# Top-k attentions: a chunk's negated maxima transposed and added one chunk's step sooner than its weights

## The chip, the cores and the metric

The kernel runs on one core of a Trainium2 chip. Times are device microseconds of one execution. The kernel before was run three times: 2546.03 us is the median, 2543.44 and 2556.37 us are the ends. One execution was profiled, and it has a time of its own.

## What is computed

Eight sequences of 256 tokens with 128 features go through four layers. Each layer adds a gated cross-attention and a gated feed-forward part to `x`:

```python
x = x + tanh(g_xattn[n]) * xattn_n(layernorm(x), ctx)
x = x + tanh(g_ffn[n])   * ffn_n(layernorm(x))
```

The cross-attentions are, in order: a causal linear attention with random features (block 0), an attention with 8 heads of 64 that keeps the 64 largest of 256 scores of a query (block 1), a full attention with 16 heads of 8 (block 2), and an attention with 16 heads of 8 that keeps the 32 largest of 256 scores (block 3). The feed-forward parts are a full attention beside eight linear experts (block 0), gated experts (block 1), eight experts with GELU and a shared one (block 2), and an attention whose projections are mixtures of 16 experts (block 3). The change touches the two attentions that keep the largest scores:

```python
sim = q @ k.T * scale                       # per head: 256 queries x 256 keys
keep = the k largest of each query          # k = 64 (block 1), 32 (block 3)
attn = softmax(where(keep, sim, -inf))
out = attn @ v
```

## The kernel before

The 2048 tokens are worked on in four groups of 512 (two sequences each). The program is emitted by two Python generators side by side. `largest_scores` emits block 1's cross-attention and then block 3's, for all four groups. `others` emits all the other blocks in the list that `stages` gives. A group's part of block 3's attention may start only when `block2_ffn` has finished that group (`middle`), and block 1's only when `block0_ffn` has (`started`). The last feed-forward blocks (`block3_ffn`) follow block 3's attention.

Both attentions are emitted by `attention_largest`. It works in chunks: a sequence's heads are split in four, so there are 32 chunks for each of the two attentions. For chunk k there are these steps:

- `fetch` (L412) multiplies queries and keys on PE (L420), with queries on the partitions, and copies the scores from PSUM into SBUF on ACT (L427).
- The search finds out which scores are dropped. In block 3 (`largest`, L376) DVE takes the eight largest of a row (L385) and replaces them (L389), four times over for each of eight rows of heads and query halves, which is 32 maxima and 24 replacements in a chunk. POOL takes the first maximum with its sign changed (L387) and makes a mask of what lies below the last one (L392). In block 1 a threshold is found by counting signs on ACT (`count`, L495), and DVE picks from what lies near it (`keep_largest`, L536 to L558), one step later.
- `weigh` (L563) makes the weights with keys on the partitions. First `shifted` brings the negated maxima to where they are needed. In block 3 (L1378) two transposes on PE put them into a PSUM bank (L1382), and DVE adds them to the chunk's queries (L1383); the queries have a row for it, against which the keys hold a one. In block 1 (L1192) two products transpose them in three bf16 parts (L1198), and ACT copies them to a row in SBUF (L1204). Then PE multiplies keys and queries again (L574), adds block 1's row (L582) and subtracts the mask (L584) into the same PSUM tiles; ACT counts the mask (L592, block 3) and takes the exponential (L599); and PE multiplies with the values (L357 or L1216).

The loop at L652 emits a step k: the search of chunk k with the fetch of chunk k + 1 (`units`, L620) and, spread between its pieces, the weights of chunk k - 2, which `behind` holds. An `Ahead(steps, gen)` (L31) takes its pieces in proportion to the share of the step that is done. Before the change `weigh` yields after the shift, after the exponentials and after the products, so the shift of a chunk is emitted at the start of a step, its score products after a quarter, its output products after a half.

What is emitted is not yet the order of execution. The whole program stands in a block with `schedule_with_timeline_sim=True` (L1845): a planner with costs of its own lays out the order of each engine's instructions from the emitted order and the dependencies. Each engine then works through its own list in that order, and waits where an operand is not there.

PSUM is handed out in two kinds of tiles: four of one bank (`bank`, L110), which hold the transposed maxima among others, and two of two banks (`pair`, L113), which hold the scores of `fetch`, the weights of `weigh`, and those of blocks 0 and 2.

Other lines that the prediction names: the outputs of full attentions and of block 3's attention are divided on DVE (L347), transposed (L341 ahead of it and L324 behind it) and projected (L330); `block1_ffn` multiplies an expert's gated half (L1273) by a routing weight (L1301) on DVE and then multiplies with the second matrix on PE (L1303); the layer norm's last step is L275 on DVE and its transposes are L282; `block2_ffn` multiplies on PE at L1476 and L1445; `block3_ffn` at L1580 to L1582.

Of the kernel before, what the change touches and what calls it, by code (L numbers as in the profile page):

```python
# [30 lines left out]
class Ahead:  # L31
# [18 lines left out]
    def finish(self):  # L50
        while self.step():
            pass
        return self.value


def alongside(gen, *others):

    for f in gen:
        for o in others:
            o.up_to(f)  # L60
        yield f
    for o in others:
        o.finish()
# [27 lines left out]
def gated_blocks_kernel(ctx: ExitStack, tc: tile.TileContext, a, out):  # L91
# [9 lines left out]
    def program(exact):  # L101
# [11 lines left out]
        def pair(name="pair"):  # L113
            return psum.tile([P, 1024], F32, tag="pair", name=name, bufs=2)

        def work(name):

            return act.tile([P, 1024], F32, tag="work", name=name, bufs=4)
# [277 lines left out]
        def attention_largest(  # L396
# [9 lines left out]
            NP = R // 2  # L406
            NJ = 2 * R
            batches = [(g, bb) for g in groups for bb in range(2)]
            ready, ahead, masks, shifts, placed = {}, {}, {}, {}, {}
            n = len(batches) * 4  # L410

            def fetch(k):  # L412
# [117 lines left out]
            def keep_largest(k):  # L530
# [25 lines left out]
                for j in range(NJ):  # L556
# [3 lines left out]
                        accum_out=dropped[:, NJ * k + j : NJ * k + j + 1],  # L560
                    )

            def weigh(k):  # L563

                i, c = divmod(k, 4)
                qT, kT, va = ready[i]
                mask = masks.pop(k)
                row = shifted(shifts.pop(k), qT, c)
                yield
                sps = [pair("sw").rearrange("p (r n q) -> p r n q", r=2, n=2) for _ in range(NP)]  # L570
                for m in range(2):
                    for r in range(R):
                        rs = slice(rows * r, rows * r + rows)
                        nc.tensor.matmul(  # L574
                            sps[r // 2][:, r % 2, m, :], lhsT=kT[rs, c, m * P : (m + 1) * P], rhs=qT[rs, c, :],
                            start=(m == 0), stop=False,
                        )
                for r in range(R):
                    for m in range(2):
                        sp = sps[r // 2][:, r % 2, m, :]  # L580
                        if row is not None:
                            nc.tensor.matmul(sp, lhsT=pick[:, r : r + 1].to_broadcast([P, P]), rhs=row, start=False, stop=False)  # L582
                        for qc in range(2):
                            nc.tensor.matmul(  # L584
                                sp[:, qc * P : (qc + 1) * P], lhsT=mask[:, r, qc, m * P : (m + 1) * P], rhs=drop,
                                start=False, stop=(m == 1 and qc == 1),
                            )
                if dropped is not None and not search:

                    for h in range(NP):  # L590
                        kept = act.tile([P, NJ // NP, S], BF16, tag="s", name="kept", bufs=2)
                        nc.scalar.activation(  # L592
                            kept, mask[:, 2 * h : 2 * h + 2].rearrange("p r q k -> p (r q) k"), AF.Copy,
                            accum_out=dropped[:, NP * k + h : NP * k + h + 1],
                        )
                es = []
                for sp in sps:
                    e = work("eK").rearrange("p (r n q) -> p r n q", r=2, n=2)
                    nc.scalar.activation(e, sp, AF.Exp)  # L599
                    es.append(e)  # L600
                yield
                products(i, c, es, va)
                yield
                if c == 3:
                    yield from finish(i, *batches[i])

            behind = Ahead(0, iter(()))
# [4 lines left out]
            def look_ahead(k, share):  # L612

                i = k // 4 + 1
                if k < n and i < len(batches) and k % 4 >= first_of and i not in ready and may_start(batches[i][0]):
                    if i not in ahead:
                        ahead[i] = Ahead(9, prepare(*batches[i]))
                    ahead[i].up_to((k % 4 - first_of + share) / (last_of - first_of + 0.5))

            def units(k):  # L620
                if not search:
                    for r in range(R):
                        if k < n:
                            for u, _ in enumerate(select(k, r)):
                                yield (r + (u + 1) / (2 * rounds)) / R
                        if r == R - 2 and k + 1 < n:
                            yield from until_ready(k + 1)
                            fetch(k + 1)
                        yield (r + 1) / R
                    return  # L630
                for slot in range(4):
                    parts = []
                    if k < n:
                        if slot == 0:
                            parts.append(first(k))
                        elif slot % 2:
                            parts.append(count(k, slot // 2))
                        elif k + 1 < n:
                            yield from until_ready(k + 1)
                            fetch(k + 1)  # L640
                    if 0 < k <= n:
                        if slot % 2 == 0:
                            parts.append(count(k - 1, 2 + slot // 2))
                        elif slot == 3:
                            parts.append(keep_largest(k - 1))
                    for u in range(5):
                        for p in parts:
                            next(p, None)
                        yield (slot + (u + 1) / 5) / 4

            steps = n + 2
            for k in range(steps):  # L652
                for f in units(k):
                    if f is not None:
                        behind.up_to(f)
                        look_ahead(k, f)
                    yield None if f is None else (k + f) / steps
                behind.finish()

                done = k - 1  # L660
                if 0 <= done < n:
                    behind = Ahead(4 if done % 4 < 3 else 12, weigh(done))
            for _ in alongside((x / 12 for x in range(1, 13)), behind):
                yield 1.0

# [213 lines left out]
        for g in range(NG):  # L879
# [6 lines left out]
            for t in range(NT):  # L886
                n = g * NT + t
# [267 lines left out]
        def block1_xattn(groups, room, dropped, may_start, done):  # L1155
# [73 lines left out]
            def finish(i, g, bb):  # L1229
# [10 lines left out]
                if bb == 1:  # L1240
                    done.add(g)

            yield from attention_largest(
                groups, prepare, shift, shifted, products, finish, 64, 8, room, dropped, not exact, may_start
            )
# [122 lines left out]
        def block3_xattn(groups, weights, rounds, room, dropped, may_start, finished):  # L1368
# [25 lines left out]
            def finish(i, g, bb):  # L1394
                yield from heads_back(g, bb, oTs.pop(i), done)
                if bb == 1:
                    finished.add(g)

            yield from attention_largest(
                groups, prepare, shift, shifted, products, finish, 32, rounds, room, dropped, False, may_start  # L1400
            )
# [486 lines left out]
```

## Time and profile before

| | |
|---|---|
| median of three runs | 2546.03 us |
| profiled execution, its own time | 2546.42 us |
| its span in the profile | 2544.7 us |
| mean granted clock of TensorE | 0.862 |
| PE, matrix products busy | 2123.7 us (83%) |
| DVE busy | 1762.5 us (69%) |
| ACT busy | 1149.0 us (45%) |
| POOL busy | 879.8 us (35%) |
| block 3's maxima (L385), first and last | 1192.5 and 2347.4 us |

The span is what the profile sees; the rest of the execution's time lies around it. PE is TensorE, DVE is VectorE, ACT is ScalarE, POOL is GpSimd. In the row of slices the span is cut into 40 equal parts of 63.6 us, and a digit is the busy share of a part in tenths (9 is 90% or more). The chain is followed back from the last instruction to what released each step; a share of it tells where time was set. A line of waits has the engine and tile that waited, what it waited for, then the total in us, the times and the longest. A line of a timeline has the start, the length, the engine, line and operands, and in brackets the idle time ahead of it with what ended it. A fp32 product shows as several matrix records, so the counts of PE are higher than the counts of calls.

### The profile page before, as it was taken

What the parts mean: (1) busy time and instruction counts of PE and PEld (TensorE: products, weight loads), DVE (VectorE), ACT (ScalarE), POOL (GpSimd) and SP (SyncE); (2) the same over time, 40 slices, a digit from 0 to 9 for tenths busy, and PEclk for the clock granted to TensorE, in tenths of its full rate; (3) what the DMA queues carried; (4) which work ended last, traced back from release to release, by engine and by line L of the source; (5) the groups of instructions that cost most, each with busy time, mean ns of one, the idle gap of its engine ahead of it and who ended that gap; (6) DMA issues with size and microseconds to landing.
All of it is one profiled execution on the core that took longest, in us unless ns stands there. A gap on an engine that the chain in (4) does not pass through costs nothing.

```text
span 2544.7 us, 35734 instructions
## 1 busy us (share of the span) xinstructions
PE 2123.7 (83%) x12068; PEld 1292.4 (51%) x12094; DVE 1762.5 (69%) x5463; ACT 1149.0 (45%) x2437; POOL 879.8 (35%) x2252
## 2 busy tenths in 40 slices
PE   7998888887878778888989868899676975988898
PEld 5655455554445444445444435445343444666677
DVE  4635757756765667665899879894798869798332
ACT  2236556546554677864355433464333542322101
POOL 3104434434432464531334324341233334233000
PEclk8999889978988889998599966899775986999999
DMA  2000001000000000010001100021000110000000
GB/s 63 6 1 2 1 1 32 1 1 1 1 1 1 1 26 1 26 34 22 1 1 42 34 1 1 1 59 50 1 1 1 42 42 1 1 5 1 5 5 6
DMA packets 47896, 32.97 MB, mean 13 GB/s; under 512 B 4747, under 2 KB 42838, under 8 KB 47702
## 3 DMA queue, kind: packets, MB, share of 16 engines
q1 hardware_dynamic: 47702, 30.58, 4.2%
q8 instruction: 97, 1.59, 0.3%
q14 instruction: 97, 0.79, 0.1%
HBM read 29.53 MB, written 1.05 MB: 12 GB/s over the span
## 4 chain that ended last, share of the span: by engine, by line
DVE 39%; PE 36%; ACT 13%; POOL 8%; issue 4%; DMA 0%; DVEq 0%; SPq 0%; ACTq 0%; POOLq 0%
DVE m L385 13%; DVE wk L389 12%; ACT signs L495 4%; PE sm L687 3%; PE sw L723 3%; PE ph L1476 3%; PE pp L299 3%; PE y L1445 2%; DVE nmz L695 2%; PE po L1635 2%; ACT sign L495 2%; PE oT L357 2%; PE o L1216 2%; DVE xe L851 2%; DVE list L542 1%
## 5 line engine op out<-in xcount | busy, mean ns | idle before, releaser
L392 POOL TENSOR_SCALAR mask<-rooms,m 128x256 bf16<-128x256 f32 x192 | 223.3, 1163 | 385.5 <-DVE m L385 353.4
L385 DVE MAX8 m<-wk 128x8 f32<-128x256 f32 x768 | 326.8, 426 | 37.0 <-DVE wk L389 0.9
L723 PE MATMUL sw<-qT,kT 32*128 32x256 f32 x1024 | 172.4, 476 | 68.3 <-ACT eK L599 24.1
L695 DVE TENSOR_REDUCE nmz<-sm 128x4 f32<-128x1024 f32 x128 | 154.9, 1219 | 105.1 <-PE sm L687 96.6
L389 DVE MATCH_REPLACE8 wk<-m,wk 128x256 f32<-128x256 f32 x512 | 208.9, 408 | 0.0
L495 ACT ACTIVATE signs<-room,nt 128x256 bf16<-128x256 f32 x288 | 145.9, 507 | 128.7 <-POOL nt L527 78.5
L687 PE MATMUL sm<-kT,qT 32*128 32x256 f32 x1024 | 152.6, 440 | 40.0 <-DVE nmz L695 28.4
L592 ACT ACTIVATE kept<-mask 128x1024 bf16<-128x1024 bf16 x64 | 67.6, 1057 | 227.3 <-POOL mask L392 227.1
L1476 PE MATMUL ph<-xnT,we 128*128 128x512 f32 x288 | 156.2, 638 | 15.5 <-ACT hT L1477 7.4
L723 PEld LDWEIGHTS sw<-qT,kT 32*128 32x128 f32 x1024 | 101.0, 222 | 128.4 <-DVE nmz L695 32.3
L737 ACT ACTIVATE eT<-sw 128x1024 f32<-128x1024 f32 x128 | 129.6, 1019 | 79.9 <-PE sw L723 73.9
L574 PE MATMUL sw<-qTk,kTk 32*128 32x256 f32 (+1 forms) x768 | 120.8, 456 | 53.6 <-DVE qTk L1383 35.2
L1445 PE MATMUL y<-hT,we 128*128 128x512 f32 x288 | 146.0, 620 | 0.6 <-DVE wb_sb L1457 0.6
L687 PEld LDWEIGHTS sm<-kT,qT 32*128 32x128 f32 x1024 | 92.3, 205 | 101.0 <-DVE nmz L695 42.9
L1477 ACT ACTIVATE hT<-ph,b 128x512 f32<-128x512 f32 x144 | 98.4, 686 | 98.8 <-PE ph L1476 94.4
L599 ACT ACTIVATE eK<-sw 128x1024 f32<-128x1024 f32 x96 | 96.6, 1019 | 89.4 <-PE sw L584 88.5
L420 PE MATMUL sp<-kTk,qTk 32*128 32x256 f32 (+1 forms) x768 | 121.1, 448 | 14.8 <-ACT eT L737 6.5
L357 PE MATMUL oT<-eT,va 128*32 128x256 f32 x1024 | 120.6, 449 | 10.2 <-ACT eT L737 9.3
L392 POOL TENSOR_SCALAR mask<-room,m 128x256 bf16<-128x256 f32 x64 | 74.5, 1164 | 155.2 <-DVE m L385 152.8
L574 PEld LDWEIGHTS sw<-qTk,kTk 32*128 32x128 f32 (+1 forms) x768 | 71.5, 212 | 96.1 <-issue 42.4
L420 PEld LDWEIGHTS sp<-kTk,qTk 32*128 32x128 f32 (+1 forms) x768 | 72.5, 209 | 59.5 <-issue 17.0
L387 POOL TENSOR_SCALAR nmk<-m 128x1 f32<-128x1 f32 x256 | 59.5, 232 | 100.7 <-DVE m L385 100.6
(381 smaller groups left out, 4976.2 us busy)
## 6 DMA issues: line engine op xcount, KB each, us to landing
we<-in_L_ffn_exp_w_dram SPq DMA_DIRECT2D x64, 256.0 KB
we<-in_L_ffn_shared_w_dram SPq DMA_DIRECT2D x8, 256.0 KB
x<-in_x_dram SPq DMA_DIRECT2D x4, 256.0 KB
big_ctx<-in_ctx_dram SPq DMA_DIRECT2D x4, 256.0 KB
w1f<-in_L_ffn_fc_w_dram SPq DMA_DIRECT2D x1, 1024.0 KB
w3a<-in_L_ffn_q_proj_dram SPq DMA_DIRECT2D x4, 256.0 KB
w3a<-in_L_ffn_k_proj_dram SPq DMA_DIRECT2D x4, 256.0 KB
w3b<-in_L_ffn_v_proj_dram SPq DMA_DIRECT2D x4, 256.0 KB
```

The costliest lines, as they stand in the source:

```text
L357: nc.tensor.matmul(o[32 * r : 32 * r + 32, :], lhsT=va[:, n, 4 * c + r, :], rhs=es[r // 2][:, r % 2, n, :], start=(n == 0), stop=(n == 1),)
L385: nc.vector.max(m8, src[:, j, :])
L389: nc.vector.match_replace(wk[:, j, :], m8, src[:, j, :], LOWEST)
L392: nc.gpsimd.tensor_scalar(mask[:, j, :], s[:, j, :], m8[:, 7:8], 1.0, ALU.is_lt, ALU.mult)
L420: nc.tensor.matmul(sps[r // 2][:, r % 2, qc, :], lhsT=qT[rs, c, qc * P : (qc + 1) * P], rhs=kT[rs, c, :], start=(qc == 0), stop=(qc == 1),)
L495: nc.scalar.activation(to, s[:, j, :], AF.Sign, bias=nt[:, j : j + 1], accum_out=acc[:, j : j + 1])
L574: nc.tensor.matmul(sps[r // 2][:, r % 2, m, :], lhsT=kT[rs, c, m * P : (m + 1) * P], rhs=qT[rs, c, :], start=(m == 0), stop=False,)
L687: nc.tensor.matmul(sps[r // 2][:, r % 2, j, :], lhsT=qT[rs, 2 * cp + j, qc * P : (qc + 1) * P], rhs=kT[rs, 2 * cp + j, :], start=(j == 0), ...
L695: nc.vector.tensor_reduce(nmz[:, qc, 2 * cp : 2 * cp + 2, 2 * h : 2 * h + 2, 8].rearrange("p c r -> p r c"), sps[h], AX.X, ALU.max, negate ...
L723: nc.tensor.matmul(sps[r // 2][:, r % 2, n, :], lhsT=kT[rs, c, n * P : (n + 1) * P], rhs=qT[rs, c, :], start=(n == 0), stop=(n == 1),)
L1445: nc.tensor.matmul(y, lhsT=w2[:, c, :], rhs=hs[c // 2][:, js], start=(c == 0), stop=(c == 3))
L1476: nc.tensor.matmul(pp[:, js], lhsT=w1[:, c * P : (c + 1) * P], rhs=xnT, start=True, stop=True)
```

## The change

A new function `shift_scores` calls `shifted` for the chunk whose search has just ended, one step before its weights. The loop calls it once the share of the step is over 0.6, or at the end of the step. `weigh` no longer calls `shifted` and no longer yields behind it, so `Ahead` counts 3 pieces (11 at the end of a sequence) instead of 4 (12): the score products of the chunk come at the start of the following step, the output products after a third. The operations and their operands stay the same.

```diff
+            def shift_scores(k):
+
+                if 0 <= k < n:
+                    i, c = divmod(k, 4)
+                    rows_of[k] = shifted(shifts[k], ready[i][0], c)
+
             def weigh(k):
 
                 i, c = divmod(k, 4)
                 qT, kT, va = ready[i]
                 mask = masks.pop(k)
-                row = shifted(shifts.pop(k), qT, c)
-                yield
+                shifts.pop(k)
+                row = rows_of.pop(k)
...
             for k in range(steps):
                 for f in units(k):
                     if f is not None:
+                        if f > 0.6 and k - 1 not in rows_of:
+                            shift_scores(k - 1)
                         behind.up_to(f)
                         look_ahead(k, f)
                     yield None if f is None else (k + f) / steps
+                if k - 1 not in rows_of:
+                    shift_scores(k - 1)
                 behind.finish()
 
                 done = k - 1
                 if 0 <= done < n:
-                    behind = Ahead(4 if done % 4 < 3 else 12, weigh(done))
+                    behind = Ahead(3 if done % 4 < 3 else 11, weigh(done))
```

More of the change, by code (lines that the diff above doesn't have):

```diff
@@ L408, in attention_largest @@
             batches = [(g, bb) for g in groups for bb in range(2)]
-            ready, ahead, masks, shifts, placed = {}, {}, {}, {}, {}
+            ready, ahead, masks, shifts, placed, rows_of = {}, {}, {}, {}, {}, {}
             n = len(batches) * 4
```

## The prediction

> **What bounds the kernel now.** I read the page first (shares and slices, then the chain), then the waits of the matrix engine, then stretches of the span, then the matrix engine's timeline where it stood idle.
>
> ```profile
> span 2544.7 us, 35734 instructions
> PE 2123.7 (83%) x12068; PEld 1292.4 (51%) x12094; DVE 1762.5 (69%) x5463; ACT 1149.0 (45%) x2437; POOL 879.8 (35%) x2252
> ...
> PE   7998888887878778888989868899676975988898
> ...
> DVE  4635757756765667665899879894798869798332
> ...
> DVE m L385 13%; DVE wk L389 12%; ACT signs L495 4%; PE sm L687 3%; PE sw L723 3%; PE ph L1476 3%; PE pp L299 3%; PE y L1445 2%; DVE nmz L695 2%; PE po L1635 2%; ACT sign L495 2%; PE oT L357 2%; PE o L1216 2%; DVE xe L851 2%; DVE list L542 1%
> ```
>
> No engine is the bound throughout. Up to 1140 us (18 slices of 63.6) PE is mostly 80 to 90% busy and the chain is mixed. From 1192 us, where block 3's search starts, the chain changes hands: a group's eight chunks of maxima run at DVE's pace (slices at 8 and 9; L385 and L389 are a quarter of the whole chain), then the next group waits until block 2's experts (`block2_ffn`), on PE, have finished it. The gaps in DVE's maxima show it: 1450 to 1482, 1729 to 1797, 2039 to 2071 us, each ahead of a new group.
>
> ```profile
> PE sw L574 <- DVE qTk L1383: 35.2, 8, 10.6
> PE pt_o L324 <- DVE o_sb L347: 33.0, 13, 8.2
> ```
>
> The first line is what the change aims at: block 3's weight products waited eight times, 35.2 us in all, for the addition of the shift. PE takes its products in order, so all behind them waits as well. The largest, at 1490.8, 1806.0 and 2078.5 us, are 10.6, 9.0 and 7.4 us, the last chunks of groups 0, 1 and 2.
>
> **The change, part by part.** No operation is added or removed. 64 transposes (L1382) and 32 additions (L1383, 0.41 us) of block 3, and 64 products (L1198) and 32 copies (L1204, 0.34 us) of block 1, are emitted at 0.6 of the step before; the weights lose one of their paces, so scores, mask products and exponentials come a quarter step sooner, the outputs a sixth. No DMA moves, POOL gets nothing new. A planner then sets each engine's order, and that of the changed program can be read without running it. To price places in it I count the instructions ahead and use the trace of before: one maximum with its share of the replacement costs 0.84 us (chunk 16, 1797.5 to 1824.4 us, 26.9 us for 32).
>
> (1) *The waits aimed at.* The additions of chunks 7, 15 and 23 pass only 4, 3 and 4 maxima (278 to 274 ahead, 533 to 530, 785 to 781), while their weights on PE stay: 3.4, 2.5 and 3.4 us of 27.0, since these chunks' shift comes at 0.6 of a step whose maxima can't start sooner. The other five waits are 8.2 us together; most go. So at most some 16 of 35.2 us. And what follows takes it back:
>
> ```profile
> 1525.25 0.47 PE L324 MATMUL pt_o<-ident,o_sb 128*128 128x128 f32 x1 [8.18 <-DVE o_sb L347]
> ```
>
> 24 us after the 10.6 us wait PE waits again, for an output in DVE's queue with 307 maxima ahead of it (306 in the new order). DVE is 88% busy from 1480 to 1530 us (44.1 of 50), so a PE that comes 3.4 us sooner waits 3.4 us longer. Bounds -16 and 0; I take -2, near the lower end of the gain, because two of the three large waits lie in such stretches.
>
> (2) *A new lag in group 0.* The price of the change is in the vector queue. In the new order block 3's maxima of chunks 2 to 5 stand ahead of other work there: the last eight multiplications by routing weights (L1301) of `block1_ffn` for group 2 have 114 to 142 maxima ahead instead of 94 to 121 (17 to 24 more), the normalization (L275) of `block2_ffn` for group 1 has 161 instead of 137 to 139. At 0.84 us that is 14 to 20 us; with what else changed places, each at its own row's mean, 12 to 19; I take 15. PE's order hardly moves there (those products L1303 have -2 to +5 us more PE work ahead), and in before it arrives with nothing to spare:
>
> ```profile
> 1297.73 1.12 PE L1303 MATMUL y<-h,w1f 128*128 128x512 f32 x2 [0.22 <-DVE h L1301]
> ...
> 1323.42 1.88 PE L1303 MATMUL y<-h,w1f 128*128 128x512 f32 x2 [2.50 <-DVE h L1273]
> ```
>
> The same place shows in block 3's own weights: for chunks 2, 3 and 4 they come 4 to 16 us of PE work sooner while the additions come 2 to 5 us of DVE work later, which turns 0.2 to 2.8 us to spare into lacks of 8 to 16. These are one lag, not several: PE runs 15 us ahead of DVE there and has to give that up once. Behind it in PE's queue is `block2_ffn` of group 1, whose end opens block 3's group 1.
>
> ```profile
> 1282.00:1325.00 43.00, 38.51 (x163) 18.87 (x164) 41.25 (x152) 20.26 (x28) 14.13 (x23) 0.94 0.00 1
> 1325.00:1480.00 155.00, 142.86 (x688) 73.40 (x689) 129.30 (x389) 81.05 (x124) 56.62 (x78) 0.93 0.11 31
> 1697.00:1797.00 100.00, 94.79 (x473) 50.69 (x472) 53.56 (x121) 51.34 (x80) 20.66 (x24) 0.97 0.13 38
> 1960.00:2057.00 97.00, 91.66 (x315) 41.75 (x317) 63.51 (x215) 50.75 (x73) 34.31 (x47) 0.92 0.20 55
> ```
>
> (Stretch, length, then busy us of PE, weight loads, DVE, ACT, POOL; then the granted clock.) From 1325 to 1480 us PE is idle for 12.1 of 155 us, so it can win back little: bounds 0 (all absorbed) and +15; I take +12 at the start of group 1 (1482 us in before).
>
> [...]
>
> ```profile
> 1480.00:1490.80 10.80, 10.20 (x98) 5.59 (x90) 7.87 (x26) 4.99 (x5) 3.79 (x7) 1.00 0.01 2
> 1490.80:1501.40 10.60, 0.04 (x2) 0.03 (x1) 9.77 (x33) 3.23 (x5) 4.07 (x6) 0.67 0.00 0
> 1501.40:1512.00 10.60, 9.86 (x47) 5.84 (x47) 9.74 (x33) 2.40 (x4) 4.07 (x6) 0.50 0.00 0
> ```
>
> After 10.6 us of waiting the granted clock was 0.50 for at least the next 10.6: 9.86 us of work that takes 4.93 at full clock, 4.9 us lost. [...]
>
> (3) *A gain in group 2.* The outputs of `block2_xattn` for group 3 (L347) and the normalization of its experts (L275) pass 10 maxima: 701 to 691 ahead, 8.4 us. PE waits there for both (5.33 and 3.63 us below, 0.91 and 1.75 between them), and 94% of the stretch behind it (1960 to 2057) is PE work that opens group 3.
>
> ```profile
> 1947.95 0.47 PE L324 MATMUL pt_o<-ident,o_sb 128*128 128x128 f32 x1 [5.33 <-DVE o_sb L347]
> ...
> 1960.46 1.38 PE L282 MATMUL pt_ln<-ident,xn 128*128 128x128 f32 x4 [3.63 <-DVE xn L275]
> ```
>
> Bounds -8.4 and 0, since the outputs also need transposes (L341) that PE issues no sooner; I take -5.
>
> (4) *Block 1.* Its three waits for the row copy (4.2 us) go, covered by more work between copy and use; mask products come up to 16 us nearer to the masks (L558), which 14 of them already waited for (8.3 us). Bounds -4 and +8, taken at 0: products of scores and searches keep their places. One more activation-table load in all (1.28 us) lies on ACT, 45% busy; uncovered it would cost its length.
>
> (5) *The last group.* The fetch of chunk 26 falls behind 14 of the first 16 experts of `block3_ffn` for group 0: 42 products of about 0.43 us are 18 us of delay for that chunk. In before the next chunk has such a gap (2158.8 to 2180.7 us), and in the new order it goes, as chunk 27's fetch keeps its place. Taken at 0, bounds 0 and +18. The products after 2350 us keep their order to 4 us.
>
> Sum: -2 + 12 - 5 + 0 + 0 = +5. On the profiled execution's own 2546.42 us (span 2544.7, 1.7 around it) that is 2551.4; this execution stands 0.4 above the median of the three runs, 2546.03. I say 2551.
>
> **The rivals.** *Slower, by one mechanism:* the lag of (2) is paid whole and with the half clock. 19.9 us, nothing won back, is about 2566. For it: PE's 92% from 1325 us on. Against it: 12 us of idle there, and (3). It decides from 12.7 us on. *Faster:* PE's waits go and the next groups really open sooner: -16 from (1), -8 from (3), and only 6 of the lag remains: 2528. For it: PE is 92 to 95% busy ahead of each opening. Against it: 8.18 us at 1525. *The change does nothing,* since the three large waits stay: 2546; for it, DVE's order of maxima itself moves by 1% at most. It counts with my own case.
>
> **How the numbers follow.** 0.5%, 12.7 us, is about what a measurement of this kernel can tell from no change. My case, with the one that nothing happens: 0.38, its own range 2540 to 2558. Slower: 0.37, 2559 to 2590, with (4) and (5) at their upper ends. Faster: 0.25, 2515 to 2533. 2524 to 2580 leaves out a tenth at each end.
>
> **What would show it.** Right: waits of L574 for L1383 fall to about 20 us, with those of chunks 7, 15 and 23 still there; PE waits more for L1301 or L1273 around 1285 to 1340 us; group 1's first maximum some 10 us later than 1482, group 3's within 6 us of 2071. Wrong: group 1 starts at or before 1482, or the time from 2071 to the end (473 us) moves by more than 8 us.

## The result and the profile after

| | before | after |
|---|---|---|
| median | 2548.71 us (7 runs) | 2562.33 us (7 runs, 2555.25 to 2570.18) |
| ratio, 95% interval | | 1.0051 (1.0033 to 1.0068) |
| span of the profiled execution | 2544.7 us | 2560.6 us |
| its mean granted clock | 0.862 | 0.861 |

The changed kernel is slower by 0.5%, 13.6 us between the medians; the prediction said 5 us. Its range (2524 to 2580) holds the time, but the range is wide: 2562.33 us lies outside that of the prediction's own case (2540 to 2558) and in that of its slower rival (2559 to 2590). In the changed kernel the lines of `weigh` are six further down (L574 is L580) and those behind the loop ten (L1383 is L1393); in the variants with a condition it is thirteen and seventeen. The page of the changed kernel answers to the one of before:

```profile
span 2560.6 us, 35742 instructions
PE 2111.6 (82%) x12067; PEld 1290.8 (50%) x12094; DVE 1760.7 (69%) x5463; ACT 1150.9 (45%) x2438; POOL 878.7 (34%) x2252
...
PE   7999789788878778888689968899776966778898
...
DVE  4535767856754767655999679894789766997332
...
DVE m L385 12%; DVE wk L389 11%; ACT signs L495 6%; PE y L1455 3%; PE sm L697 3%; PE ph L1486 3%; PE pp L299 3%; PE sw L733 3%; ACT sign L495 2%; PE o L1226 2%; PE po L1645 2%; DVE nmz L705 2%; PE pqk L1590 2%; PE pqk L1591 2%; PE pv L1592 2%
```

The work is the same, DVE's maxima still lead the chain, and `block3_ffn`'s products (L1590 to L1592) have come into its list: this fits time that has gone to the last group. The waits of PE in the changed kernel (total, times, longest):

```profile
PE o L1226 <- ACT eK L605: 38.5, 17, 4.2
PE pt_o L324 <- DVE o_sb L347: 29.4, 13, 7.7
...
PE sw L580 <- ACT rooms L427: 19.6, 4, 8.3
...
PE sw L580 <- DVE qTk L1393: 5.4, 3, 3.5
```

The wait that the change aims at fell from 35.2 to 5.4 us by its name. It did not go, though: 19.6 us now stand under the copy of fetched scores (L427), which was not among the weights' costly waits before. All waits of L574 (L580 after), whatever for, went from 53.5 to 47.7 us. And in block 1 the output products wait 38.5 us for the exponentials (L1216: 14.6 before).

The first maximum of a chunk marks the stages (us from the start of the span, one execution each):

| first maximum of | before | after | difference |
|---|---|---|---|
| chunk 0 (end of block 1's search) | 1192.5 | 1196.8 | +4.3 |
| chunk 8 (group 1) | 1482.3 | 1489.9 | +7.6 |
| chunk 16 (group 2) | 1797.5 | 1807.6 | +10.1 |
| chunk 24 (group 3) | 2071.1 | 2075.6 | +4.5 |
| chunk 26 | 2127.9 | 2154.8 | +26.9 |
| chunk 27 | 2180.7 | 2187.7 | +7.0 |
| last maximum ends | 2347.4 | 2357.5 | +10.1 |
| span | 2544.7 | 2560.6 | +15.9 |

Group 2 gives 5.6 us back; from group 3's first maximum to the end 473.6 us have become 485.0, and PE's busy time there is about the same, so it is idle for 98.0 us instead of 85.0 (before's line first):

```profile
2071.10:2544.70 473.60, 388.59 (x2206) 305.59 (x2206) 302.31 (x903) 97.06 (x194) 97.91 (x160) 0.89 0.01 3
```

```profile
2075.60:2560.60 485.00, 387.04 (x2206) 304.50 (x2206) 302.74 (x903) 97.07 (x193) 98.15 (x160) 0.88 0.01 3
```

That is the place that the prediction took at nothing. Its waits of PE (from 2181 us in before, 2188 us in the changed kernel, to the last maximum) show new names. The changed kernel:

```profile
PE pt_e L1620 <- ACT e L1616: 9.0, 2, 8.1
...
PE s L1603 <- ACT qT L1598: 8.1, 1, 8.1
PE sw L580 <- DVE xe L861: 6.6, 2, 4.6
```

In before the first was 5.4 us, the second 1.3, the third absent. These earlier stretches of the changed kernel answer to those shown of before (stretch, length, then busy us of PE, weight loads, DVE, ACT, POOL; then the granted clock):

```profile
1325.00:1480.00 155.00, 142.17 (x661) 72.27 (x660) 123.24 (x393) 83.89 (x124) 54.79 (x77) 0.96 0.11 31
1490.00:1499.00 9.00, 8.37 (x80) 4.76 (x78) 8.34 (x29) 3.06 (x3) 3.79 (x7) 1.00 0.01 3
1499.00:1506.70 7.70, 0.02 (x2) 0.02 (x2) 7.08 (x24) 2.12 (x4) 2.72 (x4) 0.74 0.00 0
1507.00:1518.00 11.00, 9.53 (x47) 5.45 (x45) 10.10 (x34) 1.83 (x2) 5.11 (x7) 0.50 0.00 0
```

The wait of chunk 7's weights is still in its place, 8.3 us instead of 10.6, and half clock follows it for 11 us again. These lines of PE's timeline answer to the last ones shown of before:

```profile
1329.25 1.12 PE L1313 MATMUL y<-h,w1f 128*128 128x512 f32 x2 [0.78 <-DVE h L1311]
...
1532.33 0.47 PE L324 MATMUL pt_o<-ident,o_sb 128*128 128x128 f32 x1 [7.73 <-DVE o_sb L347]
...
1964.35 1.24 PE L282 MATMUL pt_ln<-ident,xn 128*128 128x128 f32 x4 [5.09 <-DVE xn L275]
```

PE is held up for L324 at 1532 us as it was at 1525, as step (1) said. L1313 (L1303 before), where step (2) looked for the lag, hardly waits. The product behind the layer norm, step (3)'s place, waits longer by its name (5.09 us for 3.63), but it comes sooner: 156.7 us after group 2's first maximum instead of 162.9.

### The profile page after: what moved, and what is told of

Its sections match the earlier page's. It is cut to its first block, busy times and chain, and to the rows that moved or that the text cites. A ratio compares the mean times of both kernels' runs of the same rounds, so it can differ in the third digit from the quotient of the medians.

```text
span 2560.6 us, 35742 instructions
## 1 busy us (share of the span) xinstructions
PE 2111.6 (82%) x12067; PEld 1290.8 (50%) x12094; DVE 1760.7 (69%) x5463; ACT 1150.9 (45%) x2438; POOL 878.7 (34%) x2252
## 4 chain that ended last, share of the span: by engine, by line
PE 39%; DVE 35%; ACT 14%; POOL 8%; issue 4%; DMA 0%; DVEq 0%; SPq 0%; ACTq 0%
DVE m L385 12%; DVE wk L389 11%; ACT signs L495 6%; PE y L1455 3%; PE sm L697 3%; PE ph L1486 3%; PE pp L299 3%; PE sw L733 3%; ACT sign L495 2%; PE o L1226 2%; PE po L1645 2%; DVE nmz L705 2%; PE pqk L1590 2%; PE pqk L1591 2%; PE pv L1592 2%
## 5 line engine op out<-in xcount | busy, mean ns | idle before, releaser
L385 DVE MAX8 m<-wk 128x8 f32<-128x256 f32 x768 | 327.0, 426 | 35.8
L733 PE MATMUL sw<-qT,kT 32*128 32x256 f32 x1024 | 162.6, 464 | 34.8 <-DVE nmz L705 13.4
L697 PE MATMUL sm<-kT,qT 32*128 32x256 f32 x1024 | 153.1, 441 | 39.7 <-DVE nmz L705 25.8
L598 ACT ACTIVATE kept<-mask 128x1024 bf16<-128x1024 bf16 x64 | 67.6, 1056 | 248.9 <-POOL mask L392 248.8
L580 PE MATMUL sw<-qTk,kTk 32*128 32x256 f32 (+1 forms) x768 | 123.2, 473 | 47.8 <-ACT rooms L427 19.6
L733 PEld LDWEIGHTS sw<-qT,kT 32*128 32x128 f32 x1024 | 95.8, 214 | 85.9 <-issue 21.1
L357 PE MATMUL oT<-eT,va 128*32 128x256 f32 x1024 | 109.5, 449 | 15.2 <-ACT eT L747 10.9
L580 PEld LDWEIGHTS sw<-qTk,kTk 32*128 32x128 f32 (+1 forms) x768 | 73.1, 222 | 92.0 <-ACT rooms L427 24.6
```

Source lines behind the costliest of these rows:

```text
L385: nc.vector.max(m8, src[:, j, :])
L580: nc.tensor.matmul(sps[r // 2][:, r % 2, m, :], lhsT=kT[rs, c, m * P : (m + 1) * P], rhs=qT[rs, c, :], start=(m == 0), stop=False,)
L697: nc.tensor.matmul(sps[r // 2][:, r % 2, j, :], lhsT=qT[rs, 2 * cp + j, qc * P : (qc + 1) * P], rhs=kT[rs, 2 * cp + j, :], start=(j == 0), ...
L733: nc.tensor.matmul(sps[r // 2][:, r % 2, n, :], lhsT=kT[rs, c, n * P : (n + 1) * P], rhs=qT[rs, c, :], start=(n == 0), stop=(n == 1),)
```

## The experiments

Two theories went into the runs. *Places:* each loss belongs to a place in the order (a lag in group 0, the last group), and a variant that restores the order there has its time back. *No place:* the planner draws all orders anew whenever the emission moves, and no part of the loss can be assigned. A condition on the chunk chose in most variants where the emission is new. Each has the form of this one, with another line in `new`:

```diff
+            def new(k):
+                return search or k < 24          # search: block 1
...
-                row = rows_of.pop(k)
+                if k not in rows_of:
+                    shift_scores(k)
+                    row = rows_of.pop(k)
+                    yield
+                else:
+                    row = rows_of.pop(k)
...
-                        if f > 0.6 and k - 1 not in rows_of:
+                        if f > 0.6 and new(k - 1) and k - 1 not in rows_of:
...
-                    behind = Ahead(3 if done % 4 < 3 else 11, weigh(done))
+                    behind = Ahead((3 if new(done) else 4) + (0 if done % 4 < 3 else 8), weigh(done))
```

### The two halves of the step

The shift sooner, the weights at their old pace (against the changed kernel):

```diff
                 row = rows_of.pop(k)
+                yield
...
-                    behind = Ahead(3 if done % 4 < 3 else 11, weigh(done))
+                    behind = Ahead(4 if done % 4 < 3 else 12, weigh(done))
```

> The transposes and additions are emitted at 0.6 of the step before, as in the changed kernel, but the weights keep their old pace (a pause ahead of the score products, four pieces instead of three). In the order that results, the last eight multiplications L1301 of group 0's time have 101 to 125 maxima ahead (94 to 121 before, 114 to 142 in the changed kernel), and the fetch of chunk 26 stands ahead of all experts' products of block3_ffn, as before. Theory A (each loss has its place: a lag in group 0 and the fetch of chunk 26 behind the experts, both brought by the earlier weights): group 1 starts 2 to 5 us later than before, the time from group 3's first maximum to the end stays within 5 us of the 473.6 before, ratio 0.998 to 1.003. Theory B (any new emission shuffles all queues, and the loss has no place of its own): ratio 1.003 to 1.008, the last group again 8 to 15 us longer.

Measured: 1.0108 (1.0092 to 1.0124), 2576.47 us. Both theories named less. Group 3's first maximum to the end took 481.7 us, 8.1 more than before (the first theory had 5 at most, the second 8 to 15). The weights sooner, the shift with them:

```diff
-                shifts.pop(k)
-                row = rows_of.pop(k)
+                row = shifted(shifts.pop(k), qT, c)
```

(and the calls of `shift_scores` gone.)

> The weights come at the changed kernel's pace (no pause behind the shift, three pieces), but the transposes and additions are emitted with them, not a step sooner. L1301 has 118 to 147 maxima ahead (114 to 142 in the changed kernel), the layer norm of block2_ffn's group 1 has 169 (161), its group 3 has 704 (691 in the changed kernel, 701 before), and the fetch of chunk 26 stands behind the first experts, as in the changed kernel. Theory A: all the losses and none of the gain of group 2: group 1 starts 8 to 14 us later than before, group 3's first maximum 10 to 16 us later, the last group 8 to 14 us longer, ratio 1.006 to 1.011. Theory B: ratio between 1.001 and 1.006, with no relation to these places. A third possibility, that the earlier additions are what costs: ratio at or below 1.001.

Measured: 1.0119 (1.0104 to 1.0135), 2578.96 us, against at most 1.011 in the first theory. Its places were missed: group 1 started 28.9 us later than before (8 to 14 expected), and the last group took 475.0 us, 1.4 more (8 to 14 expected), although this kernel has both the late fetch of chunk 26 and the early weights there.

Each half alone costs twice what both cost together, so they are not two costs that add. For the weights alone about half of the loss stands ahead of block 3, in one execution: it starts at 1215.2 us, 15.6 later than the mean of six executions of the old order in block 1 (1199.6). Block 1's waits of PE (218 to 1195 us) in this run, whose L581 is the product with the row:

```profile
PE sw L581 <- ACT row_parts L1203: 11.8, 7, 6.0
```

In before it is 4.2 us and in the changed kernel 0.9: there the earlier shift pays for the earlier weights. For the shift alone no single place is found. Its profiled execution (2563.82 us) is near the changed kernel's time, its median 13 us above; the granted clock of its five runs was 0.845 to 0.852, against 0.861 to 0.867 in the runs of before beside it. Why its clock is the lowest stays open.

### One block, one group at a time

> The change for block 3's attention alone; block 1's keeps its old emission. L1301 has 94 to 122 maxima ahead, as before (94 to 121), so the lag of group 0 is left to the layer norm of block2_ffn's group 1 (145 to 147 instead of 137 to 139, that is 7 us); the fetch of chunk 26 stands behind the experts. Theory A: group 1 starts 2 to 6 us later than before, the last group is 8 to 14 us longer, ratio 1.003 to 1.006; block 1's half of the change is worth 2 to 6 us of loss through the order in group 0. Theory B: ratio 0.998 to 1.008, group 1's start anywhere within 10 us.

`return not search`: 1.0049 (1.0035 to 1.0063), as the first theory had it. Group 0 took 283.4 us from its first maximum to group 1's, as with the old order; group 1 323.0 us (314.5 to 315.3 in four executions of the old order); group 3's first maximum to the end 484.3 us.

> The change for block 1's attention alone; block 3 keeps its old emission. The order in block 3's group 0 still moves: L1301 has 106 to 133 maxima ahead (94 to 121 before), the layer norm of block2_ffn's group 1 151 to 153 (137 to 139); the last group's order is as before but for small shifts. If the losses have their places: block 3 starts 0 to 5 us later than before, group 1 4 to 10 us later, group 3 to the end within 4 us of 473.6, ratio 1.001 to 1.004. If block 1's half and block 3's half make up for each other only together (as the two parts of the step did): 1.005 to 1.012.

`return search`: 1.0021 (1.0007 to 1.0036), in the first range. Block 3 starts at 1194.6 us and group 1 at 1487.3, 2.1 and 5.0 us later than in before, as expected. But group 3's first maximum to the end takes 481.5 us, 7.9 more than before (4 at most expected), although only a few instructions of DVE, ACT and PE stand in another place there. So that stage alone can differ by some 8 us where the order is nearly the same.

Group 0 takes 292.7 us, as long as in the changed kernel, but not for the same reason: PE is idle for 39.4 us in it, 51.3 in the changed kernel, at a granted clock of 0.83 and 0.87. In the first 100 us, where the changed kernel is idle for 36.3 us, block 1's half alone has 25.6, block 3's alone 19.8, and five executions of the old order have 12.1 to 22.0. So block 1's half, which moves L1301 behind 106 to 133 maxima, seems to bring a part of the lag, and only both together bring all of it. The whole (1.0051) can't be told from both halves' product (1.0070), given the intervals.

> The change everywhere but in block 3's last group (chunks 24 to 31), which keeps the old emission. The fetch of chunk 26 still stands behind 12 of block3_ffn's first products, since what comes ahead of it is the same as in the changed kernel. Theory A, first form (what costs in the last group is the fetch behind the experts and the masks' count ahead of the queries' copies on ACT): nothing is won back, the time from group 3's first maximum to the end is 480 to 488 us, ratio 1.003 to 1.007. Second form (what costs there is the earlier weights, which take the PSUM pairs and PE from block3_ffn): 471 to 477 us, ratio 0.999 to 1.002.

`return search or k < 24`: 1.0038 (1.0025 to 1.0052). From group 3's first maximum to the end 478.0 us, between the two forms of the expectation; the ratio is the first form's. PE's idle time in this stretch is 85.5 us, as in before (85.0).

> The change for block 3's group 2 alone (chunks 16 to 23). All orders up to group 2 are as before, so this run also shows how far the starts of groups 1 and 2 differ between two executions of the same order; the fetch of chunk 26 stands behind 12 of block3_ffn's products, as in the changed kernel, and the last group's emission is the old one. If the late fetch is what costs in the last group: from group 3's first maximum to the end 481 to 486 us, ratio 1.002 to 1.005. If not: 471 to 477 us, ratio 0.998 to 1.001.

`return not search and 16 <= k < 24`: 1.0000 (0.9988 to 1.0011); 477.8 us to the end, and 276.0 us to the last maximum, in which before took 276.3. The late fetch of chunk 26 (the chunk starts 27 us later in this run too) costs nothing by itself, as the prediction had it.

> The change for block 3's last group alone (chunks 24 to 31). The fetch of chunk 26 stands ahead of block3_ffn's products, as before, while the maxima ahead of block3_ffn's own reductions are the changed kernel's (913 and 979 instead of 903 and 971). If the last group's earlier weights are what costs: from group 3's first maximum to the end 480 to 486 us, ratio 1.002 to 1.005. If the late fetch is what costs: 471 to 477 us, ratio 0.998 to 1.001. All orders up to group 3 are as before, so the starts of groups 0 to 3 show again what differs between executions of one order.

`return not search and k >= 24`: 0.9995 (0.9979 to 1.0010), 477.7 us to the end. Nor do the last group's own early weights.

> The change for block 3's groups 2 and 3 alone (chunks 16 to 31). By themselves the two groups' changes cost nothing (1.0000 and 0.9995), and from group 3's first to the last maximum they took 276.0 and 274.5 us (276.3 before; 281.9 in the changed kernel). Together they have the changed kernel's last group: the fetch of chunk 26 behind 12 of block3_ffn's products, and the masks' counts on ACT one place further ahead of the copies of block3_ffn's queries. If the two only cost where they meet: 281 to 284 us from group 3's first to the last maximum, ratio 1.002 to 1.004. If the costs add: 274 to 278 us, ratio 0.998 to 1.001, and the last group's loss in the changed kernel comes from what lies ahead of it.

`return not search and k >= 16`: 1.0029 (1.0017 to 1.0041), 283.9 us to the last maximum and 485.4 to the end. Two parts that cost nothing alone cost 0.3% where they meet. From group 3's first maximum on the order of every engine is the changed kernel's, and so are the waits, under this kernel's line numbers (2170 us to the last maximum):

```profile
PE pt_e L1627 <- ACT e L1623: 9.0, 2, 8.1
PE sw L587 <- DVE xe L868: 7.9, 2, 5.6
PE s L1610 <- ACT qT L1605: 7.2, 1, 7.2
```

> The whole change but for chunk 23 of block 3, which keeps the old emission. That puts the fetch of chunk 26 ahead of block3_ffn's products again, as before, while the weights of the last group stay early, and the order in groups 0 and 1 is the changed kernel's. If the last group costs only where the late fetch and the early weights meet: 274 to 278 us from group 3's first to the last maximum (281.9 in the changed kernel), group 1 5 to 8 us later than before as in the changed kernel, ratio 1.001 to 1.004 (the changed kernel: 1.0051). If the last group's loss has another cause: 281 to 284 us, ratio 1.004 to 1.006.

`return search or k != 23`: 0.9983 (0.9968 to 0.9997). One chunk's old emission turns a loss of 0.5% into no loss. Neither range held this: 17 us lie between that and the changed kernel's loss, and the last group's length gives 4 of them (480.8 us for 485.0), so where most of them come from is not shown. In the last group the waits for the queries' copies (L1605) and nearly all those for the PSUM pair (xe) are gone:

```profile
PE pt_e L1627 <- ACT e L1623: 12.2, 2, 7.5
...
PE sw L587 <- DVE xe L868: 1.8, 1, 1.8
```

The stretch to the last maximum stayed at 283.3 us all the same, which speaks against the expectation's first form; but PE's idle time from group 3's first maximum to the end fell from 98.0 to 86.7 us, which speaks for it. The granted clock of that stretch was 0.87, and 0.88 in the changed kernel. The order up to group 3's start is the changed kernel's, yet this execution came there 7.6 us sooner; so part of the difference of the two profiles is not of the edit.

What most of these kernels' orders have in common with their waits is DVE's queue. PE's idle time from 100 us after group 3's first maximum to the last maximum, summed from its records, stands here against the number of maxima that `block3_ffn`'s second and third reductions of a softmax's maximum (L1603 before, L1613 after) have ahead:

| kernel | second, third reduction | PE idle, us |
|---|---|---|
| before; block 1 alone | 903, 971 | 23.5; 22.3 |
| w_only | 903, 979 | 26.8 |
| mid_only; last_old; g2_only; early_and_mid | 906, 973 | 25.0; 24.7; 29.8; 22.7 |
| without the counts (below) | 907, 978 | 30.5 |
| all_but_23 | 909, 975 | 27.1 |
| s_only | 911, 977 | 25.3 |
| block3_only; g3_only | 913, 979 | 30.6; 32.9 |
| after; g2_g3 | 913, 982 | 37.7; 38.6 |

At 0.84 us a maximum the ten and eleven places are 8.4 and 9.2 us for the two reductions; in the changed kernel they start 10.0 and 10.9 us later after group 3's first maximum than in before. The exponentials, transposes and products of that attention wait behind them. This is read from orders and traces side by side. No run moved the reductions alone, so it is argued, not shown, and s_only doesn't fit: nearly as many places, and hardly more idle time than before. Idle time there isn't all lost either, since the last group alone has 9 us more of it and the time of before.

### ACT's queue

In the changed kernel two large waits of PE, one in group 0 and one in the last group, end with a copy or an exponential on ACT that stood behind a count of the mask (L598), which itself waited for POOL. On ACT:

```profile
1280.02 1.06 ACT L598 ACTIVATE kept<-mask 128x1024 bf16<-128x1024 bf16 x1 [9.77 <-POOL mask L392]
...
1281.08 1.92 ACT L605 ACTIVATE eK<-sw 128x1024 f32<-128x1024 f32 x2
...
2301.76 1.06 ACT L598 ACTIVATE kept<-mask 128x1024 bf16<-128x1024 bf16 x1 [10.60 <-POOL mask L392]
...
2303.08 0.36 ACT L1598 COPY qT<-pqk 128x256 f32<-128x256 f32 x1
```

and on PE:

```profile
1282.13 1.07 PE L357 MATMUL oK<-eK,va 128*32 128x256 f32 x4 [8.64 <-ACT eK L605]
...
2303.49 0.79 PE L1603 MATMUL s<-qT 128*128 128x256 f32 x1 [8.10 <-ACT qT L1598]
```

So the count seemed to be the cause, and the last run takes it out:

```diff
-                if dropped is not None and not search:
-                    for h in range(NP):
-                        kept = act.tile([P, NJ // NP, S], BF16, tag="s", name="kept", bufs=2)
-                        nc.scalar.activation(kept, ..., AF.Copy, accum_out=dropped[...])
...
+            nc.vector.memset(dropped[:, 128:192], 4 * (S - 32.0))
```

> The changed kernel without the 64 counts of block 3's masks on ACT (L598, 1.06 us each, 67.6 us in all, which also stood waiting for POOL's masks for 248.8 us); the counts that the last test reads are filled with the value it looks for, so ties of block 3 go unnoticed. Emission and order are otherwise the changed kernel's in the last group: the fetch of chunk 26 behind 12 of block3_ffn's products, early weights. If the last group's loss comes from ACT's queue (a count that waits for POOL, with the copies of block3_ffn's queries and the scores of the next chunks behind it): PE's wait for the queries' copies (8.1 us in the changed kernel) is under 2 us, its waits for copied scores (19.6 us for L580) are under 10 us, PE's waits from 2170 us to the last maximum are 25 to 32 us (some 38 in the changed kernel, 28 before), ratio to before 0.990 to 0.999. If ACT's queue has no part in it: those waits stay, under other names, at 36 us or more, and the ratio is 1.002 to 1.006.

Measured: 1.0056 (1.0034 to 1.0079). The wait for the queries' copies went, and most of L580's for copied scores went too, as the expectation's first form had it (of L580's waits for L427 7.4 us are left of 23.8); the kernel's time stayed where it was, as in the second. PE's waits from 2170 us to the last maximum were 35.2 us, between the two forms. Group 3 starts 9.6 us later here, though, and over the table's stretch PE is idle for 30.5 us, 37.7 in the changed kernel: half of the excess over before (23.5) went, in a group that took 484.2 us to the end all the same (485.0). Nor does the run take out the counts alone: from group 3's first maximum on PE's order is the changed kernel's, but DVE's is not (907 and 978 maxima ahead of the reductions instead of 913 and 982). Two of PE's waits over the whole span of this kernel:

```profile
PE sw L580 <- DVE qTk L1385: 25.8, 6, 7.6
...
PE pt_e L1612 <- ACT e L1608: 21.6, 8, 7.1
```

The waits for the additions are back: 25.8 us, against the 25.0 of the changed kernel's two lines together (19.6 and 5.4). In the changed kernel the copy behind the count had their name. In group 0 it is the same (first maximum of chunk 0 to that of chunk 8):

```profile
PE pt_mk L1384 <- POOL nmk L387: 12.0, 1, 12.0
PE pn L341 <- DVE x L290: 11.4, 1, 11.4
PE pg L1271 <- DVE h L1275: 11.1, 2, 10.5
```

Not one of the changed kernel's large waits there (10.5, 8.6, 5.4 us) has kept its name and size, but PE's idle time in group 0 is 52.0 us, and 51.3 in the changed kernel. In group 0, then, the count was only the last link of a chain that is late anyway; the waits that came in its place end with DVE, or with POOL's first maximum, which DVE gives. As the cause of the whole loss the theory of ACT's queue fell, since the time stayed; that ACT's queue has a part in the last group's idle time is not excluded.

### Versions that beat both

> The change for block 3's groups 1 and 2 alone (chunks 8 to 23); block 1 and groups 0 and 3 keep the old emission. In the resulting order L1301 (94 to 121 maxima ahead) and the layer norm of block2_ffn's group 1 (137 to 139) stand where they stood before, group 3's has 691 as in the changed kernel, and the fetch of chunk 26 stands behind 12 of block3_ffn's products as in the changed kernel. If the losses sit in group 0 and in the last group's own emission, and the gain in group 2: group 1 starts within 4 us of before, group 3's first maximum 2 to 8 us sooner than before (2071), ratio 0.996 to 1.000. If the late fetch of chunk 26 is what costs in the last group: the time from group 3's first maximum to the end is 8 to 12 us longer than before (473.6) and the ratio 1.000 to 1.003. If the loss has no place of its own: 1.003 to 1.008 like the others.

`return not search and 8 <= k < 24`: 0.9968 (0.9956 to 0.9981), 2544.63 us against 2551.22 of before beside it. Group 2 takes 267.3 us from its first maximum to group 3's (273.6 before), and 474.4 us follow to the end. The ratio is in the first range, and the last group is not longer though its fetch of chunk 26 is late. The starts of groups 1 and 3 in the profiled execution, the slowest of the eight, missed theirs (8.7 and 5.5 us later than before).

> The change where it costs nothing by the runs so far: in block 1 for the chunks 0 to 7 alone, in block 3 for the chunks 8 to 21 alone. L1301 (94 to 121 maxima ahead) and the layer norm of block2_ffn's group 1 (137 to 139) stand as before, that of group 3 has 693 ahead (701 before, 691 in the changed kernel), and the fetch of chunk 26 stands ahead of block3_ffn's products as before. If gains and losses have their places: group 1 within 4 us of the runs with the old order in group 0 (1478 to 1491), from group 2's first maximum to group 3's 266 to 270 us (273.6 before), ratio 0.994 to 0.998. If each new emission is a new draw: anywhere between 0.997 and 1.010.

`return (search and k < 8) or (not search and 8 <= k < 22)`: 0.9944 (0.9923 to 0.9965), 2543.98 us against 2556.63. Group 2 takes 268.0 us, group 3's first maximum to the end 474.0. Group 1's start (1484.7 us), group 2's length and the ratio are all in the first range. With the loss in group 0 and that of the last group left out, the change is worth half a per cent.

## Why the prediction was right or wrong

Where several kernels share an order up to a point, their profiled executions give the length of a stage more than once. Old order: before, mid_only, g2_only, g3_only, g2_g3 (and block3_only for block 1), each as far as it is unchanged. New order: after, last_old, all_but_23 (for block 1 b1_only and the kernel without the counts too, for the last group g2_g3).

| stage | old order, us | new order, us | measured | predicted |
|---|---|---|---|---|
| to chunk 0, step (4) | 1192.5 to 1204.4, mean 1199.6 (6) | 1190.0 to 1204.3, mean 1196.0 (5) | -3.6 | 0 |
| group 0, step (2) | 277.2 to 289.8, mean 285.2 (5) | 293.1 to 295.0, mean 293.8 (3) | +8.6 | +12 |
| group 1, step (1) | 314.6 to 315.4, mean 315.1 (4) | 317.7 to 319.3, mean 318.3 (3) | +3.2 | -2 |
| group 2, step (3) | 273.5, 273.6 (2) | 265.3 to 268.2, mean 267.2 (3) | -6.4 | -5 |
| group 3's start to the end, step (5) | 473.6 (1) | 485.0, 485.4 (2) | +11.6 | 0 |

They sum to +13.4, the medians differ by 13.6. So close an agreement is luck: against block 1 alone (481.5 us, nearly the old order) the last stage would be +3.7. PE's idle time tells the last stage better: 85.0 and 87.1 us in before and block 1 alone, 98.0 and 98.7 in the two executions of the new order.

- *Step (5) failed:* it took the last group at 0. Its reason about the fetch held (g2_only: 1.0000). What it left out is that the last group's early weights change DVE's and ACT's order for `block3_ffn` as well; the text looked at PE's order and at the fetch alone. The two together cost (g2_g3: 1.0029), with 14 us more of PE's idle time before the last maximum. Why they do is open: the reductions' places are argued, and with the shift at its old place (w_only) both are there and the group takes 475.0 us. A sign of being wrong that the prediction named, "moves by more than 8 us", came true. The bounds 0 and +18 held it.
- *Step (2) was right in size, wrong in place.* The lag of 15 us: PE's idle time in group 0 is 31.2 to 39.9 us in the five executions of the old order, 35.8 in the mean, and 50.2 to 51.3 in the three of the new one, 50.8: 15.0 more. The stage became 8.6 us longer (+12 taken). But it came between 1203 and 1294 us, under other names than L1301; from 1285 to 1340 us, where the prediction expected them, the waits for L1301 and L1273 hardly grew (3.7 to 4.4 us). The claim that the several lacks are one lag is borne out by the run without the counts. The places ahead of L1301 don't price it alone: s_only has 101 to 125 and 46.7 us of idle time in group 0, block 1 alone 106 to 133 and 39.4.
- *Step (1)* said that at most 16 us of waits go and that the next wait takes the gain back. 5.8 us went of all that L574 waits, and the wait for L347 stayed (7.7 us for 8.2). That those for the addition would remain at about 20 us is wrong by the name (5.4), right by the place: chunk 7's and chunk 15's are still there with 8.3 us each, as waits for L427, and chunk 23's with 3.5, still for the addition, which makes 20.1 (27.0 before). Without the counts they are waits for the addition again, of 6.7, 6.7 and 1.7 us. Group 1 became longer, not shorter.
- *Step (3)* held, place and size: -5 predicted, -6.4 measured. In all five kernels whose layer norm of `block2_ffn` for group 3 has 691 or 693 maxima ahead, group 2 takes 265.3 to 268.2 us; in the eight with 701 or more, 271.2 to 276.7 (block 3 alone has 697 and 265.4). g2_only is among these (701, 276.4 us), though its weights in group 2 are early: the gain goes with the order, not with the early weights themselves. The 701 and 691 are the layer norm's alone; the outputs (L347) had 687 to 695 ahead and have 673 to 683, 11 to 14 fewer, and their waits did not shrink.
- *Step (4):* a gain of block 1 is not shown: the two ranges overlap nearly whole, and 0 fits. The waits for the row went (4.2 to 0.9 us), and new ones for the exponentials came (14.6 to 38.5 us), which its text did not name.
- *The clock:* the row came again. After the 8.3 us wait the granted clock was 0.50 for 11 us with PE 9.53 us busy, as it was 0.50 for 10.6 us with 9.86 us busy after the 10.6 us wait in before. The 19.9 us of the slower rival are the lag's 15 and the 4.9 that the prediction worked out from that row, an estimate for one such wait; no run shows the two as one loss, and group 0 became 8.6 us longer.
- *The rivals:* "slower" priced the lag whole at 2566; the time lies near it, but group 0 gave 8.6 us of it and the last group, which its case had only as an upper end, some 4 to 12. That the stages' errors made up a sum in the stated range is luck in part. "Faster" needed the openings sooner; only group 3's start, relative to group 2's, is.

## What to carry to other kernels

In a kernel whose orders a planner draws from the emission, count for each engine's queue what stands ahead of every moved instruction, in every stage, the last one too; the stage taken at nothing was the one whose other queues were not looked at. Places in a queue gave the size of a delay well where it was read in the same stage (step (3)), and did not tell which waits show it. The name of a wait is only its last link: take a link away and see whether the engine's idle time moves before calling it the cause. A change whose stages gain and lose can be kept where it gains: here 0.5% slower as a whole became 0.6% faster in part. One profile of each kernel does not tell such stages apart when one order, or nearly one, differs by 8 to 13 us in a stage: compare idle times, and several executions.

## What was not expected of the hardware

One order of instructions took 277 us in one execution and 290 in another. Before and g3_only have one order up to group 3. In the stretch that begins some 39 us after chunk 0's first maximum their windows are these, before's first:

```profile
1231.50:1266.00 34.50, 34.28 (x151) 18.33 (x152) 24.87 (x85) 12.95 (x19) 10.10 (x17) 0.51 0.00 1
```

```profile
1240.20:1274.70 34.50, 27.21 (x206) 15.74 (x205) 32.08 (x111) 16.97 (x25) 14.67 (x25) 0.90 0.00 1
```

In one the granted clock was 0.51, half clock for nearly the whole stretch, in the other 0.90. Group 0 took 289.3 to 289.8 us in three executions of this order, 277.2 and 279.8 in two; the two windows are from one execution of each kind. The same happens at the start, where before and last_old still have one order (134 to 140 us, before's first):

```profile
134.00:140.00 6.00, 6.00 (x34) 3.33 (x34) 3.32 (x4) 1.61 (x2) 0.00 (x0) 1.00 0.01 3
```

```profile
134.00:140.00 6.00, 6.00 (x16) 2.59 (x15) 2.77 (x3) 0.00 (x0) 0.00 (x0) 0.50 0.01 3
```

In both PE had waited 0.31 and 0.76 us shortly before. The clock changes at steps of 3.41 us in the records (118 stretches in before and 128 in the changed kernel, each but the last a whole number of these steps long); in last_old both waits fell into one such step (130.3 to 133.7 us), 1.07 us of idle time in all, and half clock followed for 6.8 us. In before a step ended inside the second wait (at 132.4 us), which left 0.93 us in one step, and no half clock followed; two executions give no threshold. The product behind the second wait starts at 132.55 us in before and at 132.54 in last_old, so the instructions lie at the same place and the steps do not. So the start of block 3's search is good to some 6 us either way in one profile (1192.5 to 1204.4 in six executions of one order), and only the stages that several executions share could be compared closer.
